# Edge data requested an iteration earlier, 16 single rows, eleven gather buffers and VectorE's columns by stage in a graph-network kernel

## The chip, the cores and the metric

The kernel runs on one core of one Trainium2 chip. The metric is device microseconds of one execution; 3339.4 us is the median of three runs before the change (3335.0 to 3340.0).

## The reference

One layer of a graph network: 12500 nodes with 48 features, 400000 edges sorted by destination, 32 features on each edge.

```python
h = jnp.maximum(_layernorm(x, axis=-1), 0.0)
x_i, x_j = h[dst], h[src]
tmp = jnp.concatenate([x_i, x_j, edge_attr], axis=1)
hid = jax.nn.relu(tmp @ W1 + b1)
msg = hid @ W2 + b2
return x + jax.ops.segment_sum(msg, dst, num_segments=12500)
```

## The kernel before

A first phase (`node_tables`, some 90 us) makes two tables of 128 numbers a node in HBM: `tab_a`, the destination's part of the hidden layer with its bias, and `tab_b`, the source's part. A transposed copy of the second, `bt`, stays in SBUF with one node a column.

Then `windows` goes over 391 chunks of 8 tiles of 128 edges. Edges are sorted by destination, so a chunk touches a short span of nodes: `SPANS` gives 16 nodes for chunks under 78, 32 under 165, 48 under 250, 64 under 340, 80 for the rest. These are the stages of the text. The engines' orders are written out by hand, in the loop at the end of `windows`. In iteration c:

- `prepare(c)`: SyncE requests the data of a chunk. For an even c these are the edge features of two chunks, into one of two `lhs` buffers (L382), and the destination numbers of two chunks, broadcast over the span, into one of two `row` buffers (L386). Then come the numbers that SyncE itself needs (L308), the span's rows of `tab_a` into one of three `rhs` (L400), and 17 single rows of `tab_b` into a `gs` tile that is used some chunks later (`rows`, L325). GpSimd gathers rows of `tab_b` by indirect DMA, one instruction for a tile of 128 edges, into one of eight `gb` buffers (L407). VectorE compares `row` with the span's nodes and writes the result into `lhs` (L415); the same instruction writes counts into one of three `deg` buffers.
- `before(c - 1)` and `gathered(c - 1)`: TensorE multiplies `lhs` with `rhs` (L437) into `pre` and adds the source's part (L458).
- `hidden(c - 2)` and `fold(c - 2)`: VectorE applies relu (L475), TensorE sums the edges of each node (L485) and transposes the counts (L488). `compare(c - 1)` (L426) and `add(c - 3)` (L500) are VectorE's.
- `columns(c, part)`: the source's part of some tiles isn't gathered from HBM but copied out of `bt`, one column of 128 numbers for each edge, into `gt` tiles (L369; twelve buffers). VectorE has three parts with 24, 23 and 24 columns (20 in the last from chunk 250 on), ScalarE seven parts with 12. Ahead of each part the engine loads the column numbers into registers (L308); the loads aren't counted as busy. The columns copied in iteration c are for six chunks later (`LEAD`), so from iteration 384 on none are copied.

Where a `begin` of a segment of output nodes comes up (14 of them, `BEGINS`), VectorE clears and copies a segment, and in the next iterations TensorE multiplies the finished one with W2 and SyncE stores it.

So a tile of edges gets its source part in one of three ways: 2566 tiles by GpSimd's gathers, 460 by copied columns, 51 by SyncE's single rows.

Of the kernel before, what the change touches and what calls it, by code (L numbers as in the profile page):

```python
# [16 lines left out]
P = 128  # L17
# [23 lines left out]
RAW = 6  # L41
NRAW = RAW * T
RAW_PART = 16
SPANS = ((16, 78), (32, 165), (48, 250), (64, 340), (W, NCH))
K = W + DE
I16 = mybir.dt.int16
# [2 lines left out]

COLS = RAW
LEAD = COLS
ROWS0 = 3
END = NT // T


PARTS = (
# [3 lines left out]
)  # L62
PLACE = 47
STRIP = 156
WIDE = 250
LAST_PART = (True, 48, 20)
RPART = 17
BASE = 2 * RPART

BT0 = 16512  # L70
SEG0 = 143776
SEG_SIZE = 8 * L


AT_PLACE, AT_SEG, SEG, NEXT = 36, 37, 38, 39
WIDTH = 40
LOADED = 32
LAG = 3
DEGS = 3
SLOTS = (NCH + LAG + LEAD + P - 1) // P  # L80
BANK = 4


def tiles_of(first, part):

    n = (END - first) * part // P
    return [first + (P * (j + 1) + part - 1) // part - 1 for j in range(n)]


def parts_of(c):  # L90

    return PARTS if c < WIDE else [*PARTS[:2], LAST_PART, *PARTS[3:]]


AT = [0] * (COLS + 1)
for c in range(COLS, END):
    AT.append(AT[c] + sum(n for _, _, n in parts_of(c)))
BYCOLS = [min(c for c in range(COLS, END) if AT[c + 1] >= P * (j + 1)) for j in range(AT[END] // P)]
# [160 lines left out]
def windows(nc, tc, gp, bt, ident, idx, raw, rhss, x_t, tab_a, tab_b, dst, edge_t, w2s, b2s,  # L259
# [5 lines left out]
    with ExitStack() as es:  # L265
# [5 lines left out]
        lhss = [one.tile([P, 2, CE], F32, name=f"lhs{k}") for k in range(2)]  # L271
        for lhs in lhss:
            nc.vector.memset(lhs[:W, :, :], 0.0)
        gtp = es.enter_context(tc.tile_pool(name="gtp", bufs=3))
        gtc = es.enter_context(tc.tile_pool(name="gtc", bufs=12))
        wp = es.enter_context(tc.tile_pool(name="wp", bufs=3))
# [16 lines left out]
        gts = {}  # L293
        gss = {}
        ahead = []
        pair = []

        def group(c):

# [6 lines left out]
        def numbers(c, at, n, engine, table=last):  # L306

            return nc.values_load_multi_w_load_instructions(  # L308
                table[c % P : c % P + 1, c // P, at : at + n],
                engines=[engine], min_val=0, max_val=1 << 23,  # L310
                skip_runtime_bounds_check_because="numbers of nodes, and what is made of them",
            )[1]
# [30 lines left out]

        def columns(c, part):

            of = c + LEAD
            parts = parts_of(of)
            dve, at, n = parts[part]
            place = PLACE if at < PLACE <= at + n and c >= LAG else None
            first = AT[of] + sum(n for _, _, n in parts[:part]) if of < END else len(BYCOLS) * P  # L350
            n = max(0, min(n, len(BYCOLS) * P - first))
            engine = mybir.EngineType.DVE if dve else mybir.EngineType.Activation
            copy = nc.vector.tensor_copy if dve else nc.scalar.copy
            size = -(-n // 4) * 4 if place is None else place + 1 - at
            if not n:
                if place is not None:
                    st[c - LAG]["base"], = numbers(of, place, 1, engine, cols)
                return
            got = numbers(of, at, size, engine, cols)
            if place is not None:  # L360
                st[c - LAG]["base"] = got[place - at]
            for k, to in enumerate(got[:n]):
                j, e = divmod(first + k, P)
                if j not in gts:
                    gts[j] = gtc.tile([HID, P], F32, name="gt")
                to = to.with_bounds(
                    min_val=BT0, max_val=BT0 + 4 * (NPAD - 1), guaranteed_mod_val=0, out_of_modulus=4
                ) - BT0
                copy(gts[j][:, e : e + 1], bt8[:, bass.ds(to, 4)].bitcast(F32))  # L369

        def span(c):

            return next(w for w, last in SPANS if c < last)

        def prepare(c):
            n, w = min(T, NT - c * T), span(c)
            both = lhss[c // 2 % 2]
            lhs = both[:, c % 2, :]
            if c % 2 == 0:
                at, of = c * CE, min(2 * CE, (NT - c * T) * P)  # L380
                to = span(min(c + 1, NCH - 1))
                nc.sync.dma_start(  # L382
                    both[W:K, :, :].rearrange("k a e -> k (a e)")[:, :of], edge_t[:, at : at + of]
                )
                pair[:] = [ld.tile([W, 2, CE], I16, name="row")]
                nc.sync.dma_start(  # L386
                    pair[0][:to, :, :].rearrange("w a e -> w (a e)")[:, :of],
                    dst[at : at + of].rearrange("(o e) -> o e", o=1).to_broadcast([to, of]),
                )
            row = pair[0][:, c % 2, :]  # L390
# [9 lines left out]
            nc.sync.dma_start(  # L400
                rhs.bitcast(U8)[:w, :],
                taba8[bass.ds(base, 4 * HID * w)].rearrange("(w h) -> w h", w=w),
            )
            st[c] = dict(n=n, rows=nodes)
            gb = gp.tile([P, T, HID], F32, name="gb") if c >= RAW else None
            for t in range(n - len(COLS_OF.get(c, ())) - (c in BYROWS) if c >= RAW else 0):
                nc.gpsimd.indirect_dma_start(  # L407
                    out=gb[:, t, :], out_offset=None, in_=tab_b[:, :],
                    in_offset=bass.IndirectOffsetOnAxis(
                        ap=srci[:, c * T + t : c * T + t + 1], axis=0  # L410
                    ),
                )

            deg = degs[c % DEGS]
            nc.vector.tensor_scalar(  # L415
                lhs[:w, : n * P], row[:w, : n * P], bw[:w, c : c + 1], None,
                op0=ALU.is_equal, op1=ALU.add, accum_out=deg[:w, :1],
            )
            st[c].update(rhs=rhs, lhs=lhs, gb=gb, deg=deg)
# [121 lines left out]
        def ending():  # L541

            c, g = NCH - 1, len(BEGINS) - 1
            to, = numbers(begin(g), SEG, 1, mybir.EngineType.SP)
            before(c)
            hidden(c - 1)
            fold(c - 1)
            compare(c)
            for k in range(LAG):
                st[c - 2 + k]["base"], = numbers(  # L550
                    c + 1 + k + LEAD, PLACE, 1, mybir.EngineType.DVE, cols
                )
# [201 lines left out]
def tile_gnn_preln(  # L754
# [66 lines left out]
    gp = ctx.enter_context(tc.tile_pool(name="gp", bufs=8))  # L821

    with tc.tile_pool(name="keep", bufs=1) as keep, tc.tile_pool(
        name="ps_c", bufs=1, space=PSUM
# [211 lines left out]
```

## Time and profile before

| what | value |
|---|---|
| three runs | 3340.01, 3335.01, 3339.40 us |
| the profiled execution | 3343.1 us, span of its instructions 3341.4 us |
| granted TensorE clock | 0.835 |
| busy PE / DVE / ACT / POOL | 2830.1 / 2968.1 / 3148.4 / 2472.4 us |
| columns copied by ACT / DVE | 32176 / 26704 |
| chain that ended last | DVE 50%, ACT 28%, issue 7%, PE 7% |

PE is TensorE, DVE VectorE, ACT ScalarE, POOL GpSimd, SP SyncE; a q behind the name means the engine's sequencer, as in SPq. A group names its line, engine, operation, tiles and count, then busy time and mean duration, then the engine's idle time before it and what ended it. "Issue" is idle time in which the engine waited for nothing that the profile shows: its sequencer was at work on something else, such as loading registers. Durations of single copies overlap, so a sum of durations is more than the engine's time.

### The profile page before, as it was taken

To read this page: it belongs to the slowest core of one execution; us is meant where nothing else is said; L and a number is where in the kernel's file an instruction comes from. 1 tells how busy PE (TensorE), PEld (TensorE's weight loads), DVE (VectorE), ACT (ScalarE), POOL (GpSimd) and SP (SyncE) were. 2 spreads that over 40 slices of the span, in tenths; PEclk is the share of its full clock that TensorE was granted. 3 is DMA by queue.
4 is the path that set the end of the run, shared out by engine and by line. 5 is a ranking of instruction groups with operands and counts; after the bars stand their busy time and mean duration, and the time that the engine had idled before them with its cause. 6 is when DMAs were issued, how large, how long until landed. Compare 5 with 4: busy or idle time off the path is not lost.

```text
span 3341.4 us, 117392 instructions
## 1 busy us (share of the span) xinstructions
PE 2830.1 (85%) x15533; PEld 2311.5 (69%) x15533; DVE 2968.1 (89%) x28839; ACT 3148.4 (94%) x32279; POOL 2472.4 (74%) x2629
## 2 busy tenths in 40 slices
PE   7788888888888888888888888888888888888888
PEld 6677677776666676776666676777676766667666
DVE  7888888888888889899999899998899888999995
ACT  5899999999999999999999999999999999999990
POOL 7577777777777777777777777777777777777773
PEclk9788887888888888888888788888788888888889
DMA  6422222223333323233333333333333333333332
GB/s 211 141 76 77 77 77 77 77 79 82 85 81 83 85 82 84 80 90 89 88 87 89 88 87 89 90 95 91 90 93 93 91 95 94 95 99 101 105 102 63
DMA packets 150147, 305.37 MB, mean 91 GB/s; under 512 B 62435, under 2 KB 88693, under 8 KB 141573
## 3 DMA queue, kind: packets, MB, share of 16 engines
q0 software_dynamic: 83648, 169.51, 18.7%
q1 hardware_dynamic: 65298, 128.09, 14.2%
q14 instruction: 666, 5.46, 0.6%
q8 instruction: 131, 2.15, 0.3%
q10 hardware_dynamic: 404, 0.17, 0.0%
HBM read 281.74 MB, written 18.39 MB: 90 GB/s over the span
## 4 chain that ended last, share of the span: by engine, by line
DVE 50%; ACT 28%; issue 7%; PE 7%; ACTq 2%; DVEq 1%; DMA 1%; SPq 1%
DVE gt L369 30%; ACT gt L369 28%; DVE lhs L415 8%; DVE hid L475 8%; PE p_g L485 3%; ACTq L308 2%; DVE hot L426 2%; PE pre L437 2%; DVEq L308 1%; PE pre L458 1%; DMA row<-in_dst 1%; DVE seg L500 1%; SPq L325 1%; PE p_f L528 0%; PE p_f L529 0%
## 5 line engine op out<-in xcount | busy, mean ns | idle before, releaser
L369 ACT COPY gt<-bt 128x1 f32 x32176 | 3097.7, 187 | 65.4 <-issue 46.4
L407 POOL DMA_INDIRECT gb<-tab_b,srci x2566 | 2424.6, 945 | 808.9 <-issue 704.6
L369 DVE COPY gt<-bt 128x1 f32 x26704 | 1732.1, 144 | 259.3 <-issue 238.9
L485 PEld LDWEIGHTS p_g<-hot,hid 128*128 128x128 f32 x6250 | 836.2, 213 | 645.6 <-issue 487.0
L485 PE MATMUL p_g<-hot,hid 128*128 128x64 f32 (+4 forms) x6250 | 855.4, 293 | 474.1 <-DVE hid L475 467.3
L437 PE MATMUL pre<-rhs,lhs 112*128 112x128 f32 x6250 | 1073.0, 342 | 2.8 <-DMA out_x<-in_x_t 1.7
L437 PEld LDWEIGHTS pre<-rhs,lhs 112*128 112x128 f32 x6250 | 987.2, 248 | 50.8 <-issue 31.7
L458 PE MATMUL pre<-gb,ident 128*128 128x512 f32 (+3 forms) x1540 | 709.8, 589 | 0.0
L415 DVE TENSOR_SCALAR_CACHE_REDUCE lhs<-row,bw 64x1024 f32<-64x1024 int16 (+4 forms) x391 | 492.8, 1260 | 71.4 <-PE p_g L488 39.7
L475 DVE TENSOR_SCALAR hid<-pre 128x1024 f32<-128x1024 f32 x391 | 474.3, 1213 | 0.9 <-PE pre L458 0.9
L458 PEld LDWEIGHTS pre<-gb,ident 128*128 128x128 f32 x1540 | 314.1, 227 | 231.3 <-issue 222.9
L426 DVE TENSOR_TENSOR hot<-wnum,rel 128x512 f32<-128x512 f32 (+4 forms) x391 | 206.9, 529 | 0.5 <-PE p_g L485 0.5
L458 PE MATMUL pre<-ident,gt 128*128 128x128 f32 x460 | 136.1, 325 | 0.0
L488 PE MATMUL p_g<-ident,deg 64*128 64x64 f32 (+4 forms) x391 | 106.2, 272 | 0.0
L500 DVE TENSOR_TENSOR seg<-seg,p_g 128x128 f32 (+4 forms) x390 | 93.4, 240 | 2.1 <-PE p_g L488 1.5
L458 PEld LDWEIGHTS pre<-ident,gt 128*128 128x128 f32 x460 | 79.7, 178 | 0.0
L488 PEld LDWEIGHTS p_g<-ident,deg 64*128 64x128 f32 (+4 forms) x391 | 60.9, 156 | 19.0
L833 POOL DMA_INDIRECT xg<-in_x,srci x48 | 45.7, 953 | 15.5 <-issue 14.3
L528 PE MATMUL p_f<-seg,w2s 128*48 128x512 f32 x56 | 36.7, 743 | 2.3 <-DVE xseg L535 2.3
L529 PE MATMUL p_f<-seg,b2s 1*48 1x512 f32 x56 | 36.6, 739 | 0.0
L212 ACT COPY tab<-p_n 128x512 f32<-128x512 f32 (+1 forms) x37 | 18.4, 528 | 11.1 <-PE p_n L203 11.0
L415 DVE DVE_READ_ACCUMULATOR lhs<-row,bw 64x1 f32 (+4 forms) x391 | 28.8, 74 | 0.0
(90 smaller groups left out, 365.9 us busy)
## 6 DMA issues: line engine op xcount, KB each, us to landing
gs<-tab_b SPq DMA_DIRECT2D x6528, 0.5 KB
lhs<-in_edge_t SPq DMA_DIRECT2D x195, 256.0 KB
gb<-tab_b,srci POOLq DMA_INDIRECT x2566
row<-in_dst SPq DMA_DIRECT2D x45, 256.0 KB
row<-in_dst SPq DMA_DIRECT2D x43, 192.0 KB
row<-in_dst SPq DMA_DIRECT2D x25, 320.0 KB
row<-in_dst SPq DMA_DIRECT2D x43, 128.0 KB
tab_b<-tab SPq DMA_DIRECT2D x4, 1152.0 KB
```

What stands on the lines that cost most here:

```text
L308: return nc.values_load_multi_w_load_instructions(table[c % P : c % P + 1, c // P, at : at + n], engines=[engine], min_val=0, max_val=1 << 23,
L369: copy(gts[j][:, e : e + 1], bt8[:, bass.ds(to, 4)].bitcast(F32))
L407: nc.gpsimd.indirect_dma_start(out=gb[:, t, :], out_offset=None, in_=tab_b[:, :], in_offset=bass.IndirectOffsetOnAxis(ap=srci[:, c * T + t ...
L415: nc.vector.tensor_scalar(lhs[:w, : n * P], row[:w, : n * P], bw[:w, c : c + 1], None, op0=ALU.is_equal, op1=ALU.add, accum_out=deg[:w, :1],)
L426: nc.vector.tensor_tensor(hot[:, :n, :], wnum[:, :w].unsqueeze(1).to_broadcast([P, n, w]), rel[:, c * T : c * T + n].unsqueeze(2).to_broad ...
L437: nc.tensor.matmul(pre[:, t, :], s["lhs"][:K, t * P : (t + 1) * P], s["rhs"][:K, :], start=t % BANK == 0, stop=False, skip_group_check=True,)
L458: nc.tensor.matmul(pre[:, t:e, :].rearrange("p t h -> p (t h)"), lhsT, rhs, start=False, stop=True, is_transpose=turned, skip_group_check= ...
L475: nc.vector.tensor_scalar(h[:, :n, :], s["pre"][:, :n, :], 0.0, None, op0=ALU.max)
L485: nc.tensor.matmul(p_g[:, 0, :], s["h"][:, t, :], s["hot"][:, t, :], start=t == 0, stop=t == n - 1)
L488: nc.tensor.transpose(p_g[:, 1, :], s["deg"][:w, :], ident[:w, :w])
L500: nc.vector.tensor_add(to, to, s["p_g"])
L833: nc.gpsimd.indirect_dma_start(out=xg[:, t, :], out_offset=None, in_=x[:, :], in_offset=bass.IndirectOffsetOnAxis(ap=srci[:, t : t + 1], a ...
```

## The change

- The requests for the edge data of a pair of chunks move from `prepare` of the pair's even chunk to `prepare` of the odd chunk before it (`edges`). They wait for the same buffers as before.
- SyncE's single rows go from 17 to 16 a chunk, and a `gs` tile is used one chunk after its last row was requested instead of in the same.
- `gb` buffers go from eight to eleven: every eighth to tenth chunk of eleven takes one of three in a second pool.
- VectorE's columns go by span: 27, 24 and 24 with 16 nodes; 27, 24 and 20 with 32 and 48 nodes and in odd chunks with 64; 27, 24 and 16 in even chunks with 64, and with 80. The number of a place in the segment, which VectorE also needs, moves from the second load to the first. ScalarE's parts stay.
- Columns are copied in all iterations to 389. Up to iteration 371 they are for six chunks later, from there for ever fewer, and in iteration 389 for chunk 389.

With that 2558 tiles are gathered, 471 copied by columns and 48 made of single rows.

```diff
-COLS = RAW
-LEAD = COLS
+LEAD = RAW
...
+FEWER = 372
+def parts_of(c):
+    w = next(w for w, last in SPANS if c < last)
+    n = 24 if w <= 16 else 20 if w <= 48 or w == 64 and c % 2 else 16
+    return [(True, 0, PLACE), (True, 28, 24), (True, 52, n)] + [(False, 76 + 12 * k, 12) for k in range(7)]
+def taken_by(c):
+    return c + LEAD if c < FEWER else FEWER + LEAD + (c - FEWER) * (END - FEWER - LEAD) // (END - FEWER)
-RPART = 17
+RPART = 16
...
+        def edges(k):
+            c = 2 * k
+            at, of = c * CE, min(2 * CE, (NT - c * T) * P)
+            to = span(min(c + 1, NCH - 1))
+            nc.sync.dma_start(
+                lhss[k % 2][W:K, :, :].rearrange("k a e -> k (a e)")[:, :of],
+                edge_t[:, at : at + of],
+            )
+            pairs[k] = ld.tile([W, 2, CE], I16, name="row")
+            nc.sync.dma_start(
+                pairs[k][:to, :, :].rearrange("w a e -> w (a e)")[:, :of],
+                dst[at : at + of].rearrange("(o e) -> o e", o=1).to_broadcast([to, of]),
+            )
         def prepare(c):
...
+            if c == 0:
+                edges(0)
+            elif c % 2 and c + 1 < NCH:
+                edges(c // 2 + 1)
...
-            gb = gp.tile([P, T, HID], F32, name="gb") if c >= RAW else None
+            ring = gp if (c - RAW) % (RING + MORE) < RING else gp_more
+            gb = ring.tile([P, T, HID], F32, name="gb") if c >= RAW else None
```

VectorE's order in one iteration of the stage with 16 nodes, before; a row is a line of the code, the operation, what it writes and reads, and a count:

```order
L475 TENSOR_SCALAR hid<-pre 128x1024
L308 TENSOR_LOAD cols
L369 COPY gt<-bt 128x1 x23
L426 TENSOR_TENSOR hot<-wnum,rel 128x128
L500 TENSOR_TENSOR seg_848<-seg_848,p_g 128x2x16
L308 TENSOR_LOAD cols
L369 COPY gt<-bt 128x1 x24
L415 TENSOR_SCALAR lhs_856,deg_97<-row,bw 16x1024
L308 TENSOR_LOAD cols
L369 COPY gt<-bt 128x1 x24
```

The same place of VectorE's order with the change:

```order
L486 TENSOR_SCALAR hid<-pre 128x1024
L312 TENSOR_LOAD cols
L372 COPY gt<-bt 128x1 x24
L437 TENSOR_TENSOR hot<-wnum,rel 128x128
L511 TENSOR_TENSOR seg_848<-seg_848,p_g 128x2x16
L312 TENSOR_LOAD cols
L372 COPY gt<-bt 128x1 x24
L426 TENSOR_SCALAR lhs_856,deg_97<-row,bw 16x1024
L312 TENSOR_LOAD cols
L372 COPY gt<-bt 128x1 x27
```

The loads stand where they stood; the part ahead of `hid` has grown by three columns and the one behind it by one.

SyncE's order over one pair of chunks in the stage with 64 nodes, before:

```order
L382 DMA lhs_856<-in_edge_t 32x2048
L386 DMA row<-in_dst 64x2048
L308 TENSOR_LOAD last x2
L400 DMA rhs_86<-tab_a 64x512
L325 DMA gs<-tab_b 1x512 x17
L400 DMA rhs_87<-tab_a 64x512
L325 DMA gs<-tab_b 1x512 x17
```

The same pair's length of SyncE's order with the change:

```order
L383 DMA lhs_856<-in_edge_t 32x2048
L388 DMA row<-in_dst 64x2048
L410 DMA rhs_86<-tab_a 64x512
L329 DMA gs<-tab_b 1x512 x16
L312 TENSOR_LOAD last x2
L410 DMA rhs_87<-tab_a 64x512
L329 DMA gs<-tab_b 1x512 x16
```

The load of numbers, which stood between the `row` request and the single rows, now stands behind 16 of them, and the `rhs` behind the requests is that of the chunk before the pair.

The beginning of the same stretch of SyncE's order with the change, with the waits of each request; DMAHW and a number is one of eight semaphores for landed transfers:

```order
L383 DMA lhs_856<-in_edge_t 32x2048 [waits DMAHW1_49,PE_49]
L388 DMA row<-in_dst 64x2048 [waits DMAHW2_49,DVE_49]
L410 DMA rhs_88<-tab_a 64x512 [waits DMAHW3_49]
L329 DMA gs<-tab_b 1x512 [waits DMAHW4_49]
L329 DMA gs<-tab_b 1x512 [waits DMAHW5_49]
L329 DMA gs<-tab_b 1x512 [waits DMAHW6_49]
L329 DMA gs<-tab_b 1x512 [waits DMAHW7_49]
L329 DMA gs<-tab_b 1x512 [waits DMAHW0_49]
L329 DMA gs<-tab_b 1x512 [waits DMAHW1_49]
L329 DMA gs<-tab_b 1x512 [waits DMAHW2_49]
```

The semaphores go round: the last row, the seventh single row, waits for the one that the `row` transfer had, eight requests earlier.

More of the change, by code (lines that the diff above doesn't have):

```diff
@@ L43 @@
 RAW_PART = 16
+RING, MORE = 8, 3
 SPANS = ((16, 78), (32, 165), (48, 250), (64, 340), (W, NCH))
@@ L79 @@
 DEGS = 3
-SLOTS = (NCH + LAG + LEAD + P - 1) // P
+SLOTS = (NCH + LAG + P - 1) // P
 BANK = 4
 def tiles_of(first, part):
[L86 to L98, printed above, removed]
+    n = (END - 1 - first) * part // P
+    return [first + (P * (j + 1) + part - 1) // part for j in range(n)]
+AT = [0]
+for c in range(END):
+    AT.append(AT[-1] + sum(n for _, _, n in parts_of(c)))
+BYCOLS = [taken_by(min(c for c in range(END) if AT[c + 1] >= P * (j + 1))) for j in range(AT[END] // P)]
 COLS_OF = {c: [j for j, of in enumerate(BYCOLS) if of == c] for c in sorted(set(BYCOLS))}
@@ L295, in windows @@
         ahead = []
-        pair = []
+        pairs = {}
         def group(c):
@@ L344, in columns @@
         def columns(c, part):
-            of = c + LEAD
-            parts = parts_of(of)
+            parts = parts_of(c)
             dve, at, n = parts[part]
-            place = PLACE if at < PLACE <= at + n and c >= LAG else None
-            first = AT[of] + sum(n for _, _, n in parts[:part]) if of < END else len(BYCOLS) * P
+            place = PLACE if part == 0 and c >= LAG else None
+            first = AT[c] + sum(n for _, _, n in parts[:part]) if c < END else len(BYCOLS) * P
             n = max(0, min(n, len(BYCOLS) * P - first))
@@ L356, in columns @@
                 if place is not None:
-                    st[c - LAG]["base"], = numbers(of, place, 1, engine, cols)
+                    st[c - LAG]["base"], = numbers(c, place, 1, engine, cols)
                 return
-            got = numbers(of, at, size, engine, cols)
+            got = numbers(c, at, size, engine, cols)
             if place is not None:
@@ L373, in span @@
             return next(w for w, last in SPANS if c < last)
+        def edges(k):
[11 more added lines that the diff above has]
+            )
         def prepare(c):
             n, w = min(T, NT - c * T), span(c)
[L377 to L390, printed above, removed]
+            if c == 0:
+                edges(0)
+            elif c % 2 and c + 1 < NCH:
+                edges(c // 2 + 1)
+            lhs = lhss[c // 2 % 2][:, c % 2, :]
+            row = pairs[c // 2][:, c % 2, :]
             m = max(0, min(RPART, len(BYROWS) * P - (c - ROWS0) * RPART)) if c >= ROWS0 else 0
@@ L550, in ending @@
                 st[c - 2 + k]["base"], = numbers(
-                    c + 1 + k + LEAD, PLACE, 1, mybir.EngineType.DVE, cols
+                    c + 1 + k, PLACE, 1, mybir.EngineType.DVE, cols
                 )
@@ L977 @@
     nxt = first[np.array(BEGINS[1:] + (NCH - 1,))[of]]
-    numbers[LAG + LEAD : NCH + LAG + LEAD, AT_SEG] = seg
-    numbers[LAG + LEAD : NCH + LAG + LEAD, AT_PLACE] = SEG0 + of % 2 * SEG_SIZE - BT0
+    numbers[LAG : NCH + LAG, AT_SEG] = seg
+    numbers[LAG : NCH + LAG, AT_PLACE] = SEG0 + of % 2 * SEG_SIZE - BT0
     bases = np.pad(first, (0, -NCH % 2)).reshape(-1, 2)
@@ L988 @@
     strip = np.zeros((SLOTS * P, STRIP), np.int32)
-    for c in range(COLS, END):
+    for c in range(END):
         slot = [at + k for _, at, n in parts_of(c) for k in range(n)]
         strip[c, slot] = cols[AT[c] : AT[c + 1]]
-    strip[LAG + LEAD : NCH + LAG + LEAD, PLACE] = first
+    strip[LAG : NCH + LAG, PLACE] = first
     strip = np.ascontiguousarray(strip.reshape(SLOTS, P, STRIP).transpose(1, 0, 2))
```

15 lines of the change are left out of this document (6 added, 9 removed), and 3 rows, old and new, of the table PARTS.

## Prediction

> **What bounds the kernel now.** I read the windows first, cut where the span of a chunk's nodes changes (16, 32, 48, 64, 80 nodes). With line 415 alone they count chunks: two rows of it to a chunk. Columns: stretch, length, VectorE busy and count, granted clock, DMA share, GB/s.
>
> ```profile
> 144.30:732.60 588.30, 91.16 (x144) 0.82 0.28 76
> 732.60:1452.80 720.20, 110.20 (x174) 0.83 0.31 83
> 1452.80:2112.70 659.90, 100.39 (x158) 0.83 0.33 88
> 2112.70:2159.10 46.40, 7.62 (x12) 0.85 0.33 90
> 2159.10:2917.30 758.20, 114.63 (x180) 0.82 0.36 93
> 2917.30:3226.20 308.90, 48.46 (x76) 0.85 0.38 100
> 3226.20:3275.10 48.90, 7.64 (x12) 0.93 0.41 105
> 3275.10:3341.40 66.30, 8.58 (x14) 0.90 0.19 52
> ```
>
> Length over chunks: 588.3/72 = 8.17 us with 16 nodes, 8.28, 8.35, then 46.4/6 = 7.73 for the six iterations in which VectorE already copies 67 columns instead of 71, 758.2/90 = 8.42 with 64 nodes, 308.9/38 = 8.13 and 48.9/6 = 8.15 with 80. Four sequencers stand close to these numbers.
>
> ScalarE and GpSimd, from the groups (busy, mean ns; idle time and its cause), ScalarE's last piece from the timeline, and GpSimd's and TensorE's waits:
>
> ```profile
> L369 ACT COPY gt<-bt 128x1 f32 x32176 | 3097.7, 187 | 65.4 <-issue 46.4
> L407 POOL DMA_INDIRECT gb<-tab_b,srci x2566 | 2424.6, 945 | 808.9 <-issue 704.6
> 3258.88 2.05 ACT L369 COPY gt<-bt 128x1 f32 x21
> POOL gb L407 <- PE pre L458: 42.2, 53, 26.3
> PEld pre L458 <- DMA gb<-tab_b,srci: 8.4, 27, 0.5
> ```
>
> ScalarE needs (3097.7 + 65.4)/32176 = 98.3 ns a copy, 8.26 us for the 84 of an iteration, and is done at 3260.9, some 80 us before the end. GpSimd takes (2424.6 + 808.9)/2566 = 1.26 us a gather, 8.3 us a chunk; it waited once long for a free buffer, and TensorE waited 8.4 us in all for gathered rows. Both run just level with the others and are not what is waited for.
>
> VectorE in the first stage, its timeline over one iteration, its register loads there (least, median, longest ns) and its only wait of size:
>
> ```profile
> 440.80 1.21 DVE L475 TENSOR_SCALAR hid<-pre 128x1024 f32<-128x1024 f32 x1
> 441.98 1.48 DVE L369 COPY gt<-bt 128x1 f32 x23
> 443.38 0.28 DVE L426 TENSOR_TENSOR hot<-wnum,rel 128x128 f32<-128x128 f32 x1
> 443.58 0.18 DVE L500 TENSOR_TENSOR seg<-seg,p_g 128x32 f32 x1
> 444.83 1.55 DVE L369 COPY gt<-bt 128x1 f32 x24 [1.08 <-issue]
> 446.29 1.26 DVE L415 TENSOR_SCALAR_CACHE_REDUCE lhs<-row,bw 16x1024 f32<-16x1024 int16 x1
> 447.79 1.55 DVE L369 COPY gt<-bt 128x1 f32 x24 [0.23 <-issue]
> L308 DVEq TENSOR_LOAD <-cols x217: 1598/1641/1822, 143.9 to 732.5; - x109
> DVE gt L369 <- issue: 71.2, 103, 1.2
> ```
>
> Nothing is waited for but its own sequencer: 71.2/72 = 1.0 us an iteration passes while 24 column numbers are loaded into registers, 1641/24 = 68 ns each, three times an iteration. So VectorE paces this stage by copies and loads together, 8.17 us.
>
> SyncE with 64 nodes, its timeline over one pair of chunks, then its wait for TensorE over the run and in this stage, VectorE's wait in this stage, and the landing of one row transfer with 64 and one with 80 nodes from the chain:
>
> ```profile
> 2503.86 0.33 SPq L382 DMA_DIRECT2D lhs<-in_edge_t  x1
> 2504.28 0.49 SPq L386 DMA_DIRECT2D row<-in_dst  x1
> 2507.58 0.48 SPq L400 DMA_DIRECT2D rhs<-tab_a  x1
> 2508.16 5.61 SPq L325 DMA_DIRECT2D gs<-tab_b  x17
> 2513.93 0.47 SPq L400 DMA_DIRECT2D rhs<-tab_a  x1
> 2514.54 5.92 SPq L325 DMA_DIRECT2D gs<-tab_b  x17
> 2520.56 0.33 SPq L382 DMA_DIRECT2D lhs<-in_edge_t  x1
> SPq L382 <- PE pre L458: 69.4, 57, 7.6
> SPq L382 <- PE pre L458: 2.1, 6, 0.6
> DVE lhs L415 <- DMA row<-in_dst: 19.2, 18, 3.1
> 2504.28 4.35 DMA row<-in_dst
> 2960.07 4.93 DMA row<-in_dst
> ```
>
> A pair costs SyncE 2520.56 - 2503.86 = 16.70 us here, against 2 x 8.42 = 16.85 for the pair of chunks. Elsewhere SyncE waits for TensorE to free the lhs buffer (69.4 us over the run); here it has only 2.1 us to spare in 45 pairs. It sets this stage, and the row data come late.
>
> **The change, part by part.** Sums are made against the profiled execution, 3343.1 us (span 3341.4), which lies 3.7 above the median 3339.4.
>
> *Columns, 16 nodes.* Iterations 0 to 77 go from 71 VectorE columns to 75, and the first load takes 28 numbers instead of 24. ScalarE keeps its 84. Copies follow each other at (1.48 - 0.144)/22 = 0.061 us, taking 0.144 for a single one, the mean of the group below; four cost 0.24 us, the four loads 4 x 0.068 = 0.27, in a stage whose gaps are all load time.
>
> ```profile
> L369 DVE COPY gt<-bt 128x1 f32 x26704 | 1732.1, 144 | 259.3 <-issue 238.9
> ```
>
> Upper end 0.51 us, lower end 0.24 (all added loads under other work). The trace holds the same step downwards: 71 to 67 columns moved 8.17 to 7.73, so 0.44. I take that: 78 x 0.44 = **+34** (19 to 40). Nothing hides it: ScalarE's 8.26 and GpSimd's 8.3 then lie below 8.61, and they gain a lead that only later stages could use.
> The Trainium skill, Perfetto Trace Analysis, section Optimizing Scalar/DVE Operations, puts the overhead of a VectorE operation in SBUF at about 60 ns; the 61 ns between copies agree. By that alone four columns would cost 0.24 us and the term would be 19; the two windows show nearly twice that, so the loads must be counted with the copies.
>
> *32 and 48 nodes.* 24+23+24 copies become 27+24+20: 71 as before, with 72 numbers as before. 0; only the six iterations at 7.73 go back to 71: 6 x 0.44 = **+3**. As hid comes three copies and four loads later (3 x 0.061 + 4 x 0.068 = 0.45 us), fold does too, and lhs waits for fold through its count buffer: -3 to +10 for this, 0 taken.
>
> *64 nodes.* Off SyncE's pair go two single rows, 2 x 5.61/17 = 0.66 us, and two numbers, 0.14. But the edge and row requests now stand ahead of an odd chunk, with no load of numbers behind them. Every request on this queue waits until the one eight places earlier has landed (its semaphores go round by eight, as the order shows). The seventh single row is eight behind the row transfer. Before, the loads of 2.8 us (2504.77 to 2507.58) lay between; now the seventh is due 0.42 + 0.49 + 0.58 + 6 x 0.33 = 3.5 us after the edge request, while the row data land at 0.42 + 4.35 = 4.8. So SyncE stands up to 1.3 us, and its pair is 16.70 - 0.80 + 1.3 = 17.2: no relief, only a head start, once: the requests wait for TensorE's matmuls of c - 2 in iteration c - 1, and lhs needs them at c + 1, at most 16.8 us later, 12 after landing; I count 10. 45 x 17.2 - 10 = 764 against 758.2. If SyncE kept out of the way VectorE would set the stage: 7.73 plus two columns at 0.11 is 7.95, plus the excess that the segments cost the middle stages, (720.2 + 659.9)/166 - 8.17 = 0.14: 8.1 x 90 = 729. I take **-8** (-29 to +6), nearer to SyncE's end, as its rows are from this very stage, with the standing put at 1.0 (45 x 16.9 - 10 = 750).
> The Trainium skill, SBUF — State Buffer, section The DMA setup-cost knee, gives 2 us plus bytes over 436 GB/s; for 256 KB that is an estimate of 2.6 us by this page. The transfer would land before the seventh single row is due and this stage would get the full -29. The trace has 4.35 and 4.93 us for this broadcast, so I go by those.
> Behind SyncE's earlier wait are queued rhs of the same chunk, its 16 single rows and the next numbers; rhs is needed an iteration later, so this costs nothing while SyncE keeps up.
>
> *80 nodes.* VectorE keeps 67 columns and the first load grows by four numbers: 0 to 0.27 us. SyncE stands longer: the row data land at 0.45 + 4.93 = 5.4 us, the seventh single row is due after about 3.3: 2.1 less 0.8, against waiting time that SyncE had here. Over 44 iterations (308.9 + 48.9) -2 to +12, **+4** taken.
>
> *The last chunks.* From 3275.1 VectorE copied nothing; now it has 67 columns in six more iterations, and ScalarE its 84 in five. VectorE was busy 31.0 us in that window (the row below has every engine: PE, PEld, DVE, ACT, POOL), 4.4 a chunk; 67 x 0.11 = 7.4 more make 11.8 at most against 9.5, but most of the loads lie under its waits there: 67 x 0.061 = 4.1 makes 8.5. 0 to +8, **+2** taken. ScalarE has 389 x 84 = 32676 copies, 500 more: 3260.9 + 500 x 0.0983 = 3310, and two chunks of 8.2 us plus the closing matmuls make some 3330: a floor that my sum does not touch.
>
> ```profile
> 3275.10:3341.40 66.30, 52.29 (x312) 38.89 (x310) 31.00 (x49) 0.00 (x0) 17.18 (x18) 0.90 0.19 52
> ```
>
> *Buffers and gathers.* Three more buffers can give back TensorE's 8.4 us of waiting at most; GpSimd's eight fewer gathers (10 us) are cover, not path. 0.
>
> Sum: 3343.1 + 34 + 3 - 8 + 4 + 2 = 3378, less 3.7: **3374 us**. Own range: the first term at 19 to 40, and up to 10 more from the others, 3359 to 3390.
>
> **The rivals.** A measurement of this kernel tells about 0.2% from no change, so same is 3332.7 to 3346.1.
> 1. *SyncE is freed after all* (0.20): the lane wait does not bite, 64 nodes give -29 and 80 nodes -2. 3343.1 + 34 + 3 - 29 - 2 + 2 - 3.7 = 3347. For it: two rows fewer and the earlier request. Against it: 4.35 and 4.93 us of landing. The Trainium skill's rule on setup cost, above, speaks for it.
> 2. *Gains and losses cancel* (0.12): rival 1, with only the copies' 19 us in the first stage: 3347 - 15 = 3332, up to 3337 where SyncE gives 5 us less.
> 3. *Faster* (0.10): the four columns go into the 1.0 us of idle time that VectorE has in each iteration of the first stage, and SyncE is freed. Place: line 369 in iterations 0 to 77. It decides if the stage stays at 8.26 us or less, ScalarE's pace. Then 3343.1 + 3 - 29 - 2 + 2 - 3.7 = 3313, which is below ScalarE's floor, so 3330 + 1.7 - 3.7 = 3328. Against it: that idle time is load time, and loads are what is added.
> 4. *SyncE becomes the bound of the late stages* (0.12): it stands as computed, and late rows stop TensorE again: +6, +12 and +8, beside the 34: 3343.1 + 34 + 3 + 6 + 12 + 8 - 3.7 = 3402.
> The forecast has 0.46.
>
> **How the numbers follow.** Range 3334 to 3394: it leaves out rival 3, and the far halves of rivals 2 and 4, 0.22 in all. Faster: rival 3, 0.10. Same: rival 2 and a quarter of rival 1, 0.17. Slower: the rest, 0.73.
>
> **What would show it.** In the profile after: line 415 at 8.55 to 8.70 us a chunk in the first 78, still with nothing waited for but the sequencer (wrong if 8.3 or less); 8.2 to 8.35 with 32 and 48 nodes; VectorE's wait for row data nearly gone; SyncE waiting at its single rows for row data, over 30 us in all, mostly with 64 and 80 nodes (wrong, and rival 1, if under 10); ScalarE waiting some 10 us or more for free column tiles in the first stage. A first stage at 8.2 us would bring down the whole forecast.

## The result, and the profile after

The changed kernel takes 3446.8 us (median of four runs, 3445.6 to 3451.6), the kernel before 3337.2 on the same chip: ratio 1.0333, 95% interval 1.0315 to 1.0351. It is slower by some 110 us; the forecast was 3374 with a range to 3394. The profiled execution took 3451.6 us, 108.5 more than that of before.

The windows of the changed kernel, cut at the same chunks as before (line 426 is now the lhs line, two rows of it a chunk; columns: stretch, length, VectorE busy and count, granted clock, DMA share, GB/s):

```profile
145.50:765.00 619.50, 91.13 (x144) 0.82 0.27 75
765.00:1490.70 725.70, 110.23 (x174) 0.81 0.31 83
1490.70:2148.60 657.90, 100.39 (x158) 0.83 0.34 87
2148.60:2198.95 50.35, 7.62 (x12) 0.81 0.35 88
2198.95:2987.90 788.95, 114.63 (x180) 0.83 0.35 90
2987.90:3318.90 331.00, 48.59 (x76) 0.81 0.36 94
3318.90:3371.40 52.50, 7.65 (x12) 0.86 0.28 71
3371.40:3449.90 78.50, 8.54 (x14) 0.80 0.12 32
```

Against before, from chunk 6 on: +31.2 with 16 nodes (8.17 to 8.60 us a chunk), +5.5 with 32, -2.0 with 48, +3.9 in the six chunks that had 67 columns, **+30.8 with 64 nodes** (8.42 to 8.77), **+22.1 and +3.6 with 80**, **+12.2 in the last seven chunks**. These and 1.2 us ahead of chunk 6 make 108.5. So the loss has two parts: the first stage, as forecast, and everything from chunk 250 on (68.7 us), which was forecast to break even.

The engines' waits over the whole run, the new or grown ones:

```profile
PE pre L448 <- DMA rhs<-tab_a: 123.0, 76, 3.7
ACT gt L372 <- PE pre L469: 107.0, 65, 10.0
POOL gb L418 <- PE pre L469: 105.4, 73, 8.9
```

TensorE waits 123.0 us for `rhs`, a wait that was not in the list of before; ScalarE and GpSimd, which had the least to spare before, now stand for free buffers for over 100 us each. VectorE's wait for row data did not go (25.0 us, before 27.7). SyncE's own waits over the run, of which the first and the third are new:

```profile
SPq L329 <- DMA row<-in_dst: 119.6, 142, 2.0
SPq L383 <- PE pre L469: 82.1, 62, 6.3
SPq L329 <- DMA lhs<-in_edge_t: 63.5, 122, 1.8
```

SyncE's timeline over one pair of chunks with 64 nodes, to be laid beside the pair of before:

```profile
2699.27 0.33 SPq L383 DMA_DIRECT2D lhs<-in_edge_t  x1
2699.69 0.50 SPq L388 DMA_DIRECT2D row<-in_dst  x1
2700.30 0.53 SPq L410 DMA_DIRECT2D rhs<-tab_a  x1
2700.93 6.42 SPq L329 DMA_DIRECT2D gs<-tab_b  x16
2710.20 0.47 SPq L410 DMA_DIRECT2D rhs<-tab_a  x1
2710.78 5.28 SPq L329 DMA_DIRECT2D gs<-tab_b  x16
2716.48 0.33 SPq L383 DMA_DIRECT2D lhs<-in_edge_t  x1
```

The pair is 2716.48 - 2699.27 = 17.21 us long, against 16.70 before. Sixteen single rows take 5.28 us where nothing holds them and 6.42 behind the row request: 1.14 us of standing. The load of numbers, before between row request and `rhs`, now lies ahead of the second `rhs` (2707.4 to 2710.2), so the first `rhs` is requested 0.6 us behind the request for the row data. What that does to `rhs` is seen in the chain of waits of this stage (start, length, what):

```profile
2245.39 4.52 DMA rhs<-tab_a
...
2290.58 2.25 DMA rhs<-tab_a
```

The chain has 17 `rhs` transfers (32 KB) that were requested some 0.6 us behind a row request and 1.0 us behind an edge request (256 KB each): they took 3.9 to 5.5 us to land. The two others took 2.22 and 2.25 (1.9 to 2.8 in the chains of two later runs that have the load between and the columns of before). TensorE and VectorE wait in this stage:

```profile
PE pre L448 <- DMA rhs<-tab_a: 76.0, 44, 3.7
...
DVE lhs L426 <- DMA row<-in_dst: 18.0, 20, 2.4
```

VectorE's wait for row data is nearly what it was (19.2). SyncE's own waits with 64 nodes:

```profile
SPq L329 <- DMA row<-in_dst: 49.1, 42, 1.7
SPq L329 <- DMA lhs<-in_edge_t: 4.4, 11, 0.7
SPq L329 <- DMA rhs<-tab_a: 4.1, 7, 1.1
SPq L388 <- DVE hid L486: 2.8, 7, 0.5
...
SPq L383 <- PE pre L469: 1.3, 5, 0.4
```

The single rows stand 57.6 us for transfers that have not landed. For other engines SyncE waits only 5.9 us in 789 (2.8, 1.4, 1.3 and 0.4). So its own queue sets the pace of this stage: its 1441 single rows take 537.8 us of its timeline, 0.373 us each, against 0.333 before. TensorE feels the slow queue as a wait for `rhs`. That the longer landing of `rhs` costs time by itself is not shown, since SyncE waits for hardly anyone.

### The profile page after: what moved, and what is told of

It is laid out like the page before. It is cut to its first block, busy times and chain, and to the rows that moved or that the text cites. A ratio compares the mean times of both kernels' runs of the same rounds, so it can differ in the third digit from the quotient of the medians.

```text
span 3449.9 us, 117885 instructions
## 1 busy us (share of the span) xinstructions
PE 2851.5 (83%) x15538; PEld 2339.3 (68%) x15538; DVE 3025.1 (88%) x29747; ACT 3186.2 (92%) x32779; POOL 2467.8 (72%) x2621
## 4 chain that ended last, share of the span: by engine, by line
DVE 59%; PE 11%; issue 9%; DMA 7%; SPq 7%; ACT 3%; DVEq 2%; POOL 1%; ACTq 0%; POOLq 0%
DVE gt L372 35%; DVE lhs L426 10%; DVE hid L486 10%; SPq L329 4%; PE p_g L496 4%; PE pre L448 4%; DMA rhs<-tab_a 4%; ACT gt L372 3%; DMA row<-in_dst 3%; DVE hot L437 3%; PE pre L469 2%; DVEq L312 2%; SPq L312 2%; POOL xg L844 1%; DVE seg L511 1%
## 5 line engine op out<-in xcount | busy, mean ns | idle before, releaser
L372 ACT COPY gt<-bt 128x1 f32 x32676 | 3135.5, 187 | 163.6 <-PE pre L469 107.0
L372 DVE COPY gt<-bt 128x1 f32 x27612 | 1787.6, 144 | 313.6 <-issue 295.2
L448 PE MATMUL pre<-rhs,lhs 112*128 112x128 f32 x6250 | 1100.6, 348 | 139.2 <-DMA rhs<-tab_a 123.0
L496 PE MATMUL p_g<-hot,hid 128*128 128x64 f32 (+4 forms) x6250 | 844.6, 290 | 423.8 <-DVE hid L486 409.5
L448 PEld LDWEIGHTS pre<-rhs,lhs 112*128 112x128 f32 x6250 | 1014.0, 254 | 193.0 <-issue 153.2
```

The costliest lines, as they stand in the source:

```text
L448: nc.tensor.matmul(pre[:, t, :], s["lhs"][:K, t * P : (t + 1) * P], s["rhs"][:K, :], start=t % BANK == 0, stop=False, skip_group_check=True,)
L496: nc.tensor.matmul(p_g[:, 0, :], s["h"][:, t, :], s["hot"][:, t, :], start=t == 0, stop=t == n - 1)
```

## The experiments

Three theories of the loss from chunk 250 on. **A**: the requests' own wait. With no load behind the row request, single rows wait for data requested just before, SyncE's pair becomes longer than the other engines' two chunks, and `rhs` comes late. **B**: VectorE's columns alone (more of them, a larger first load). **C**: SyncE waits for TensorE in an earlier iteration, and what is queued behind is held up. Ratios are to the kernel before, measured with it on the same chip; the chips of this table differ by up to 7 us in it (3337 to 3344).

| kernel | median us | ratio to before | 95% interval |
|---|---|---|---|
| the change | 3446.8 | 1.0333 | 1.0315 to 1.0351 |
| early requests alone | 3455.1 | 1.0342 | 1.0324 to 1.0359 |
| the change, load between | 3398.8 | 1.0157 | 1.0134 to 1.0179 |
| the same, columns as before | 3324.4 | 0.9953 | 0.9938 to 0.9967 |
| the same, no late columns | 3304.0 | 0.9896 | 0.9879 to 0.9913 |
| no late columns, requests at the even chunk | 3309.9 | 0.9915 | 0.9896 to 0.9933 |
| no late columns, late split 27+19+20 | 3318.5 | 0.9915 | 0.9893 to 0.9937 |
| no late columns, late split 20+27+20 | 3302.9 | 0.9880 | 0.9859 to 0.9900 |
| no late columns, eight buffers | 3319.4 | 0.9929 | 0.9910 to 0.9947 |

### Early requests alone

In the kernel before, only this:

```diff
-            if c % 2 == 0:
...
+            if c == 0:
+                edges(0)
+            elif c % 2 and c + 1 < NCH:
+                edges(c // 2 + 1)
```

> The kernel before with the edges' and rows' requests moved one iteration ahead and nothing else (17 single rows, 71 and 67 columns, eight buffers). Theory A, the requests' own wait: with no load of numbers behind the row request, the seventh single row waits until the row data have landed, so SyncE's pair of chunks goes from 16.7 us to 17.2 and more; from chunk 250 on the kernel loses 50 to 80 us (64 nodes 8.42 to about 8.8 us a chunk), SyncE waits over 80 us at single rows for row data and TensorE over 80 us for rhs; 16 nodes stay at 8.17; 3385 to 3415 us. Theory B, VectorE's columns do it all (71 instead of 67 from the stage with 64 nodes on, and the larger first load): 3337 within 8 us, and no wait for rhs. Theory C, the requests wait for TensorE in an earlier iteration and hold up what is queued behind them: a loss of 20 to 80 us from all stages alike, SyncE's wait for TensorE well over 69 us, and its wait for row data under 30.

3455.1 us: this one edit alone costs as much as the whole change (1.0342 against 1.0333, the intervals overlap). Waits of this run, engines and SyncE:

```profile
PE pre L444 <- DMA rhs<-tab_a: 284.7, 121, 5.3
...
DVE lhs L422 <- DMA row<-in_dst: 99.3, 76, 5.4
```

```profile
SPq L325 <- DMA row<-in_dst: 120.7, 151, 1.5
...
SPq L380 <- PE pre L444: 14.5, 4, 7.4
```

16 nodes stay at 590.2/72 = 8.20 us; from 48 nodes on every stage loses (48 nodes +18.7, 64 nodes 808.7 against 758.2, 80 nodes 337.3 against 308.9). The marks of theory A are there, but its size was too small by 40 us, and it had the loss begin at chunk 250 and not with 48 nodes. B fails as the only cause, since the columns are those of before. C fails: SyncE's wait for TensorE is gone from here almost wholly. With 17 rows in place of 16 the late stages lose still more than in the changed kernel (with 64 nodes the single rows take 567.6 us of SyncE's timeline against 537.8): the fewer single rows were a relief there, but too small.

### The load between the row request and the rows

In the changed kernel the numbers of chunks c and c + 1 are loaded at odd c (the host lays them out accordingly):

```diff
-            if c % 2 == 0:
+            if c == 0 or c % 2:
                 ahead[:] = [
...
-            base, nodes = ahead[BASE + c % 2], ahead[c % 2 * RPART :][:m]
+            k = 1 if c and c % 2 == 0 else 0
+            base, nodes = ahead[BASE + k], ahead[k * RPART :][:m]
```

> The changed kernel with SyncE's numbers loaded at odd chunks, so that the load stands between the row request and the single rows, as it stood in the kernel before; everything else as in the changed kernel. Theory A: SyncE's wait for row data falls from 119.6 us to under 25, TensorE's wait for rhs from 123.0 to under 40; 64 nodes 8.77 to 8.45 us a chunk or less, 16 nodes stay at 8.6; 3375 to 3400 us against 3447. Theory B: 3435 to 3450, since the columns are untouched. Theory C: over 3420, the earlier wait for TensorE (82.1 us in the changed kernel) stays and rhs still comes late.

3398.8 us, 48 less (59 by the ratios). SyncE's pair with 64 nodes in this run, one half of it:

```profile
2699.15 0.33 SPq L383 DMA_DIRECT2D lhs<-in_edge_t  x1
2699.58 0.50 SPq L388 DMA_DIRECT2D row<-in_dst  x1
2703.14 0.50 SPq L411 DMA_DIRECT2D rhs<-tab_a  x1
2703.74 5.26 SPq L329 DMA_DIRECT2D gs<-tab_b  x16
...
2715.17 0.33 SPq L383 DMA_DIRECT2D lhs<-in_edge_t  x1
```

The pair is 16.02 us, the sixteen rows take 5.26 again, `rhs` comes 3.6 us behind the row request in place of 0.6. SyncE's wait for TensorE over this run:

```profile
SPq L383 <- PE pre L470: 256.0, 114, 10.4
```

SyncE now has time over. Its wait for row data is down to 0.2 us, and TensorE's for `rhs` no longer stands in the list of waits. The windows with 16, 64 and 80 nodes:

```profile
144.10:764.40 620.30, 91.15 (x144) 0.80 0.29 75
2209.85:2960.40 750.55, 114.46 (x180) 0.83 0.38 93
2960.40:3274.75 314.35, 48.46 (x76) 0.87 0.40 99
```

64 nodes go from 789.0 to 750.6, 80 nodes from 331.0 to 314.4; the first stage stays. That is theory A in place and size. The requests are as early, and SyncE's wait for TensorE (theory C) has grown, yet this loss is gone. So the early request costs by what it stands next to. The edit takes away the standing and the close `rhs` together; that the standing is what counts is read from SyncE's waits, not from a run that parts the two.

### The columns of before

Of the run before, the columns go back (first load 24 numbers, second 23 and the place, third 24, 20 from iteration 244 on); the lines that move the place are left out here:

```diff
-    w = next(w for w, last in SPANS if c < last)
-    n = 24 if w <= 16 else 20 if w <= 48 or w == 64 and c % 2 else 16
-    return [(True, 0, PLACE), (True, 28, 24), (True, 52, n)] + [(False, 76 + 12 * k, 12) for k in range(7)]
+    n = 24 if c < 244 else 20
+    return [(True, 0, 24), (True, 24, 23), (True, 48, n)] + [(False, 76 + 12 * k, 12) for k in range(7)]
```

> The load of SyncE's numbers between row request and single rows, as in the run before this one, and VectorE's columns as in the kernel before (24, 23 and 24, from iteration 244 on 20 in the third load). Theory A with the local price of four columns and their load: the first 72 periods go back from 8.62 to 8.17-8.20 us, nothing of the gain is taken back later, and the time falls by 78 x 0.44 = 34 us, from 3399 to about 3365. Rival: ScalarE's 84 copies (8.26 us) or GpSimd hold the first stage or take the lead back in a later one; then 3380 or more, with 16 nodes at 8.3 or the middle stages slower by 0.1 us a chunk.

3324.4 us: 74 less than the run before (68 by the ratios), below both ranges given, and 0.5% below the kernel before. The windows with 16, 64 and 80 nodes and of the last chunks:

```profile
145.70:733.10 587.40, 91.17 (x144) 0.82 0.31 78
2157.45:2884.60 727.15, 114.43 (x180) 0.85 0.38 95
2884.60:3185.10 300.50, 48.43 (x76) 0.87 0.41 102
3185.10:3316.60 131.50, 16.19 (x26) 0.81 0.29 72
```

The first stage gives back 32.9 us (8.16 us a chunk): the local price, and no later stage takes it back. Unexpected in this size is the rest: 64 nodes 23.4 less, 80 nodes 13.9 less, although with 80 nodes VectorE copies 67 columns either way. So theory B has a part as well, which shows once SyncE is out of the way. Its size by stage is rough: these two profiled executions lie 89 us apart, the medians 74.

### No columns for the last chunks

```diff
-    return c + LEAD if c < FEWER else FEWER + LEAD + (c - FEWER) * (END - FEWER - LEAD) // (END - FEWER)
+    return c + LEAD
...
-    AT.append(AT[-1] + sum(n for _, _, n in parts_of(c)))
+    AT.append(AT[-1] + (sum(n for _, _, n in parts_of(c)) if c < END - LEAD else 0))
...
```

> The same, and no columns for the last six chunks: copying ends six iterations before the end, as in the kernel before. What is left of the change is 16 single rows, the early requests with the load between, and eleven buffers. Theory A: the stretch from chunk 378 to the end, 131 us in the changed kernel, goes back to 115, so 12 to 18 us less than the run with late columns: 3345 to 3355; and if SyncE is then out of the way of the late stages (64 nodes at 8.2 us a chunk against 8.42), 3325 to 3340. Rival: the copies of the last iterations replace gathers that are as dear, and nothing is saved (within 5 us of the run with late columns).

3304.0 us, 1.0% below the kernel before. With 64 nodes, and from chunk 378 to the end:

```profile
2156.00:2884.70 728.70, 114.45 (x180) 0.85 0.39 95
...
3187.60:3299.60 112.00, 16.24 (x26) 0.88 0.35 86
```

The last stretch takes 112.0 in place of 131.5: the late columns cost 19.5 us, a little over what was expected, and the total fell below both ranges given. The rival is out.

### The requests back at the even chunk

The same kernel, with `edges(c // 2)` at even c and the load behind it there.

> The same again, with the edges' and rows' requests back at the even chunk that they belong to and the load behind them there: 16 single rows and eleven buffers are all that is left of the change. Theory A: SyncE's pair is 16.70 - 0.80 = 15.9 us with 64 nodes, below the 16.85 of a pair, so 64 nodes go from 8.42 to 8.2-8.3 us a chunk; the early requests give nothing that this does not give: within 6 us of the run with early requests, 3325 to 3345. Rival: what was late with 64 nodes is the row data themselves (VectorE's wait of 19.2 us there), and without early requests it stays: 10 to 20 us above the run with them.

3309.9 us, 5.9 more; the intervals overlap. So 16 rows, with the later use of a `gs` tile that goes with them, and eleven buffers make most of the gain over the kernel before. The profiled runs show 738.9 against 728.7 us with 64 nodes and 35.1 against 38.5 in the last six periods. Whether the early requests are worth 10 us or nothing isn't settled by this.

### Where VectorE's copies stand

From iteration 244 on, 68 numbers in three loads either way:

```diff
-    n = 24 if c < 244 else 20
-    return [(True, 0, 24), (True, 24, 23), (True, 48, n)] + [(False, 76 + 12 * k, 12) for k in range(7)]
+    a, b, n = ((0, 24), (24, 23), 24) if c < 244 else ((0, 27), (28, 19), 20)
+    return [(True, *a), (True, *b), (True, 48, n)] + [(False, 76 + 12 * k, 12) for k in range(7)]
```

and, for the second run, `((0, 20), (20, 27), 20)`.

> The run without late columns (16 rows, early requests with the load between, eleven buffers; 3304 us), with VectorE's copies split otherwise from iteration 244 on: 27 behind lhs and ahead of hid, 19 behind hid, 20 ahead of lhs, in place of 24, 23 and 20, with 68 numbers loaded either way and one copy fewer. Theory D, the place of the copies: what is copied between lhs and hid makes hid, fold and the next lhs late, so three copies and four numbers more there (0.45 us) cost 0.2 to 0.45 us a chunk in 128 chunks: 8.10 to 8.3-8.5 with 64 nodes, 7.97 to 8.2-8.4 with 80, 25 to 55 us in all, 3330 to 3360. Theory E, the number of copies alone counts: one fewer, 3295 to 3308, and 64 and 80 nodes unchanged or 0.1 us faster.

> The same, split the other way from iteration 244 on: 20 copies ahead of hid, 27 behind it, 20 ahead of lhs; 67 copies and 68 numbers as with 24, 23 and 20. Theory D: hid comes four copies and four numbers earlier (0.5 us); where fold's end is what lhs waits for this gives up to 0.2 us a chunk, 3285 to 3300; TensorE's wait for hid (408 us in the run without late columns) falls by over 20 us. Theory E: 3304 within 5 us.

On one chip, 3318.5 and 3302.9 us, ratios 0.9915 and 0.9880. The profiled run with 27 copies between lhs and hid, with 64 nodes:

```profile
2159.80:2906.60 746.80, 114.56 (x180) 0.82 0.38 94
```

That is 8.30 us a chunk against 8.10, and 8.21 against 7.97 with 80 nodes, with one copy fewer. But this profiled run was the slowest of its six (3328), and the median lies only 0.2% over that of 24+23+20, with overlapping intervals. Over the opposite split, on the same chip, it lies 15.6 us, and there too the intervals overlap a little (0.9893 to 0.9900). So a price for the place of the copies (theory D) is likely but not shown, and it is smaller than the one given: the run fell short of the expected 3330. The other way nothing could be measured: 0.9880 against 0.9896, and TensorE waits for hid 407.6 us against 408.4, where D wanted 20 less. E is right there.

### Eight buffers

```diff
-            ring = gp if (c - RAW) % (RING + MORE) < RING else gp_more
+            ring = gp
```

> The run without late columns with eight buffers of gathered rows instead of eleven, nothing else. As the prediction has it the three buffers are worth nothing: 3304 within 6 us, with GpSimd waiting for TensorE's buffers 30 to 100 us more and TensorE's wait for gathered rows under 15 us. Rival: the buffers carried the gain over the kernel before, and without them it is back at 3325 or more.

3319.4 us, ratio 0.9929 against 0.9896: 0.33%, 11 us, more than expected; the intervals just touch (0.9910 to 0.9913). The waits for gathered rows with eight buffers, then with eleven:

```profile
PE pre L469 <- DMA gb<-tab_b,srci: 41.1, 30, 3.0
...
PEld pre L469 <- DMA gb<-tab_b,srci: 23.7, 35, 3.4
```

```profile
PEld pre L469 <- DMA gb<-tab_b,srci: 8.9, 30, 0.5
```

64.8 us of waiting in place of 8.9. Between the two profiled runs 9 us lie in the stage with 80 nodes (312.0 against 302.9) and 11 from chunk 378 to the end (123.1 against 112.0). The reading is that GpSimd falls behind with eight buffers once the other engines run faster. Neither forecast held: the loss is more than 6 us and the rival's 3325 was not reached.

### The same questions on another chip

Four kernels were first run on a chip on which the kernel before itself takes 5394.9 us (5380 to 5407). Two were those of the first two experiments; the other two were the changed kernel with VectorE's columns 24, 23 and 24 (20 from iteration 244 on) and the changed kernel with the requests back at the even chunk.

> The kernel before with one part of the change: the edge and row requests move to the odd chunk before the pair; 17 single rows, columns and buffers stay. Theory A (lane wait: SyncE's seventh single row stands until the row data have landed, because the load of numbers no longer lies between): the pair with 64 nodes costs SyncE 16.7 + 1.3 = 18 us or a little more, with 80 nodes 17.5 or more, with 48 nodes about 16.9; the time is 3430 to 3470 us, slower even than the whole change, since the two single rows fewer are missing. Theory B (the loss with 64 and 80 nodes comes from VectorE's larger first load and its 71 columns in odd chunks): 3310 to 3340, as nothing on VectorE changes.

> The whole change, but SyncE loads its numbers for an odd chunk and the even one behind it, so that the load stands between the row request and the single rows again, while the requests stay an iteration ahead. Theory A: SyncE's waits for row and edge data at its single rows fall from 183 us to under 30, its pair with 64 nodes from 17.2 to about 15.9 us, the stages with 64 and 80 nodes go to 8.1 to 8.3 us a chunk, and the time is 3355 to 3385. Theory C (what hurts is that the earlier requests wait for TensorE to free the lhs buffer, with rhs queued behind them): nothing changes by more than 10 us, 3437 to 3457, as that wait stays where it is.

> The whole change with VectorE's columns as before (24, 23 and 24, from iteration 244 on 24, 23 and 20; the place in the second load). Both theories: the first stage falls back to 8.17 us a chunk, 30 to 34 us less. Theory A: the stages with 64 and 80 nodes stay at 8.7 us or more a chunk and the time is 3400 to 3420. Theory B: they fall back too and the time is 3335 to 3360.

> The whole change without its first part: the requests are back at the even chunk, everything else (16 single rows, columns, buffers, last chunks) stays. Theory A: SyncE's pair with 64 nodes is 16.7 - 0.8 = 15.9 us with no lane wait, the stages with 64 and 80 nodes go to 8.1 to 8.4, and the time is 3355 to 3390, close to the run with the load between; what the head start itself is worth is the difference of the two, which I expect at 0 to 10 us. Theory B: 3420 or more, since VectorE's columns stay.

In this order: ratios 1.0005 (0.9995 to 1.0015), 1.0048 (1.0037 to 1.0060), 1.0055 (1.0037 to 1.0073), 1.0044 (1.0027 to 1.0061). They do not decide between the theories, as something else sets the time there. VectorE's and ScalarE's copies in the first of these runs, at the same moment:

```profile
2522.14 0.15 DVE L369 COPY gt<-bt 128x1 f32 x1 [0.54 <-issue]
```

```profile
2522.14 0.19 ACT L369 COPY gt<-bt 128x1 f32 x1 [0.50 <-issue]
```

Again and again, as here from 2520.7 to 2524.3, both engines start one copy every 0.70 us, at the same instants, waiting for nothing but their sequencers; elsewhere a copy follows every 0.06 to 0.1 us. ScalarE's idle time of this kind is 1798.6 us in this run, against 46.4 in the profile before. A chunk takes 13 us there, which leaves room for SyncE's standing of a microsecond. What holds the sequencers was not found.

## Why the prediction was wrong, point by point

Of the 73 us that the sum missed, 38.8 lie in the stage with 64 nodes, 21.7 with 80 and 10.2 in the last chunks.

- *Columns, 16 nodes*: **right**. Forecast 8.55 to 8.70 us a chunk and +34 over 78 chunks; measured 8.60, 0.433 a chunk, 33.8 over 78. Undoing it gave 32.9 back. The waits in this stage: VectorE still waits for its sequencer alone (71.2 us before), and ScalarE for column tiles, as forecast (over 10 us).

```profile
DVE gt L372 <- issue: 82.1, 142, 1.0
...
ACT gt L372 <- PE pre L469: 14.5, 11, 2.7
```

- *32 and 48 nodes*: **right**. +5.5 and -2.0 in the stages, within -3 to +10, and +3.9 for the six chunks (forecast 3).
- *64 nodes*: **here it failed**, -8 against +30.8. The mechanism was named: no load between, so a single row stands until the row data have landed, and SyncE sets the stage. Four terms of the sum were off. The standing was taken at 1.0 us a pair; the waits listed above make 57.6/45 = 1.28 (13 us over 45 pairs). The load of two numbers fewer was to save 0.14 a pair; it takes 2.85 us in the pair shown, 2.81 before (6 us). The pair of 16.70 was one pair read for all, where the average was 16.85 (7 us). And 10 us were taken off for a head start, which a queue that sets the pace cannot give: SyncE waited 5.9 us for other engines in the whole stage. Together that is 36 of the 38.8 us. The two single rows fewer gave what was put down for them, some 30 us (90 rows of 0.333). `rhs`, of which the prediction said that it costs nothing while SyncE keeps up, came late 44 times in 45 pairs; with SyncE setting the pace that is a consequence and no term of its own. Moving the load between took 38.4 us off this stage.
- *What the freed stage would give*: -29, by 8.1 us a chunk that VectorE was to set. The changed kernel's columns with the load between give 8.34 and only -7.6. With the columns of before it is 8.08 to 8.10, -29 to -31, but there SyncE waits 5.6 us for other engines in 727, so its own pair of 16.2 us sets that pace too: that the number agrees is in part luck. The estimate counted the copies and not their place: 27 copies stand between lhs and hid and make hid and fold later. The part on 32 and 48 nodes said that hid comes 0.45 us later, and took 0 for it; with 64 and 80 nodes it was not asked. With 80 nodes, where the count of copies is the same, the columns of the change cost 13.9/38 = 0.37 us a chunk by the profiled runs once SyncE was out of the way. The split run alone shows 0.2 us with 64 nodes and less in its median, so how much is the place and how much else isn't settled.
- *80 nodes*: +4 (up to 12) against +25.7. The same failure: the standing was set against waiting time that SyncE was said to have here, but before the change it waited some 7 us for other engines in 358. With it the single rows take 0.380 us each in place of 0.330. Moving the load between took 16.7 us off.
- *The last chunks*: +2 (0 to 8) against +12.2 from 3371 on, and 19.5 by the experiment over the last 13 chunks. The window of 66.3 us was divided by seven, 9.5 a chunk; but 21.0 of it are the closing work after the last lhs, and the six periods before were 45.2/6 = 7.5 long. Against 7.5 the 8.5 to 11.8 us that were worked out give 6 to 26. The sum was fit to find it, and was held against the wrong number.
- *Buffers*: 0. In the changed kernel they were not tried alone; TensorE's wait for gathered rows is 13.1 us there, before 8.4. In the kernel without late columns they are worth some 11 us, with intervals that just touch. The bound of 8.4 us is from the pace of before.
- *The rivals*: rival 4 had SyncE as the bound and less than half of the price (26 us for the late stages, against 68.7); it had late rows stop TensorE, where the lists show late `rhs`. The Trainium skill's rule that spoke for rival 1 (SBUF — State Buffer, section The DMA setup-cost knee; an estimate of 2.6 us for the row transfer by this page) is not borne out: by it single rows would find the data landed, and SyncE stood 119.6 us for transfers that took 4.2 to 5.4 us with 64 nodes. *What would show it*: VectorE's wait for row data should have nearly gone and did not, the one mark that pointed at SyncE's being the bound.

The costs do not add: early requests alone cost 113 us by the medians, the columns 74 after the load had been moved, late columns 20; the whole change, with what the fewer rows and the buffers give back, costs 110. With 64 and 80 nodes SyncE and VectorE run side by side, and the later of them sets the pace. SyncE's wait for TensorE with 64 nodes fits that (some 20 us with the change's columns and the load between, about 2 with the columns of before), but it was not tried by itself.

The version without late columns (16 rows, early requests with the load between, eleven buffers, columns of before) beats both kernels: 3304.0 us, ratio 0.9896; with 20+27+20 columns it is 3302.9, ratio 0.9880.

## What to carry to other kernels

Moving a request ahead in a queue also moves it next to other requests: ask what stood behind it before (here 2.8 us of loads that let its data land) and what now does, and add to the queue's own time what each request behind it then waits for. Where a queue hardly waits for other engines (here 5.9 us in 789) it is the bound, every wait in it counts in full, and a head start must not be taken off. Divide a window by the periods that lie in it, without the closing work, before a new load is held against it.

## What the runs showed of the hardware

- With 64 nodes a 32 KB transfer requested some 0.6 us behind a 256 KB one, and 1.0 us behind another, on the same queue landed after 3.9 to 5.5 us (17 cases); without these neighbours after 2.2 (2 cases).
- Eight rotating semaphores on SyncE's queue make a request wait for the one eight places earlier. In the changed kernel the single rows stood 119.6 us for row data, 63.5 for edge data and 17.3 for `rhs`.
- The kernel before took 3337 to 3344 us (medians) in four sets of runs and 5395 on one chip, where VectorE and ScalarE started single copies 0.70 us apart in step (granted clock there 0.68).
